# Projection matrices of a spectral mixer: scaled by ScalarE and summed by GpSimd, with the remainder ahead of the last square

## The chip, the cores and the metric

One core of a Trainium2 chip runs the kernel. The metric is the device time of one execution in microseconds (us), the median of several runs. The engines are named PE (TensorE, matrix products; PEld is its loading of weights), DVE (VectorE), ACT (ScalarE), POOL (GpSimd) and SP (SyncE, which issues the DMAs here). GpSimd and the DMAs work on SBUF; the results of matrix products stand in PSUM and are taken from there by VectorE and ScalarE.

## What is computed

The reference is a model of four layers on an image of 56 x 56 positions, 128 channels and a batch of 2: two layers of selective scans, an attention layer with a spectral mixer behind it, and an attention layer with experts. The change touches the mixer alone (`_L2_ffn_ref`), which convolves the tokens with 16 spectral filters, multiplies each result by a matrix, and does so for prefixes of the sequence of four lengths, each with matrices of its own:

```python
def _compute_spectral(u, sigma, phi, Mpp, Mpm):
    U_plus, U_minus = _stu_conv(phi, u, PADDED_SL)
    s = sigma ** SIGMA_POW
    out = jnp.einsum('btkd,k,kde->bte', U_plus, s, Mpp)
    out = out + jnp.einsum('btkd,k,kde->bte', U_minus, s, Mpm)
    return out
...
for i, frac in enumerate((1, 2, 4, 8)):
    xi = x[:, :T // frac]
    si = _stu(xi, sigma, phi, M_u[i], M_phi_plus[i], M_phi_minus[i])
    si = jnp.pad(si, ((0, 0), (0, T - si.shape[1]), (0, 0)))
    outs.append(si)
y_soft = jax.nn.softmax((log_weights + gumbel) / TEMPERATURE)
y_hard = jax.nn.one_hot(jnp.argmax(y_soft), 4, dtype=y_soft.dtype)
weights = y_hard - jax.lax.stop_gradient(y_soft) + y_soft
stacked = jnp.stack(outs, axis=-1)
return jnp.sum(stacked * weights, axis=-1)
```

## The kernel before

The kernel does the layers one after the other. In the mixer, even and odd positions are kept apart, so that the sum and the difference of the plus and the minus matrix of a filter act on even and odd taps. The four prefix lengths give four stretches of the sequence; in the stretch that only the longest prefix reaches one matrix acts, in the next the weighted sum of two, and so on. So for each filter the kernel needs eight matrices of 128 x 128, the tile `Wm`: two (sum and difference) for each of four stretches, each a running sum of matrices that are weighted by `ws` (a scale per filter and prefix, the same in all partitions).

`matrices(f)` (L1798) builds `Wm` for filter f: two DMAs bring the plus and minus matrices into `mpm`; GpSimd adds and subtracts them (L1803, L1804) into `both`; VectorE weights and sums them in four operations of 128 x 256 (`stretch_sums`, L1869 once and L1871 three times). `mpm` and `both` have one buffer, `Wm` has four.

The stage is 32 units: two passes, in each eight pairs of filters, and for each pair of filters two units (`eo` = 0 and 1). The two units with the same filters are called a pair here. A unit (`unit`, L1726) is four squares, which are fast convolutions of blocks. Each square (`square`, L1692) makes seven products on TensorE, each into one buffer named `cv` of a PSUM pool of six (`product`); ScalarE copies two of them out (`less`, L1708), VectorE combines them by nine operations with PSUM operands (L1711 to L1722), ScalarE makes four times a half (L1720), and GpSimd adds two halves (L1724). The squares are u0 from ("T", "A"), u2 from ("A", "A") and ("T", "B"), S from ("C", "C") and u1 from ("D", "D"). GpSimd then adds S to u2 (L1744) and to u1 (L1753). `project` multiplies a block by `Wm` on TensorE (L1823, tile `pj`, two buffers), and VectorE adds the result to `A` (L1829). The projection of u0 is written after the S square; those of u2, of the remainder's result and of u1 are left to the next unit (`waiting`, `finish`).

In the units with `eo` = 0 the `remainder` (L1765) follows: 26 matmuls of x with the last taps `H` (L1771) for both units of the pair, into one more `cv` buffer, and a copy by ScalarE into `rest` (L1776). It is written behind the D square.

`coming()` calls `matrices` for the next pair of filters in the unit with `eo` = 1, but a scheduler in the framework sets the order of each engine's instructions from what is ready: in the built program the work for the next pair stands in the unit with `eo` = 0, as soon as `Wm` buffers are free. Each engine then works through its own queue in that order. `inputs` (L1613) makes the transformed inputs vT, vA, vC and vD by VectorE, at the start and again at the change of pass; GpSimd makes part of their sources (L1630, L1632). `windows` (L1672) and `taps` load what the next units need.

Of the kernel before, what the change touches and what calls it, by code (L numbers as in the profile page):

```python
# [14 lines left out]
F32 = mybir.dt.float32  # L15
BF16 = mybir.dt.bfloat16
AF = mybir.ActivationFunctionType
ALU = mybir.AluOpType
# [6 lines left out]
C = 128  # L25
# [1564 lines left out]
class Mixer:  # L1590
# [135 lines left out]
    def unit(self, f0, eo, after, later, project, ready, coming):  # L1726

        nc = self.k.nc
        u0 = self.block("u0")
        self.square(u0, ("T", "A"))  # L1730
        self.finish(1)
        u2 = self.block("u2")
        self.square(u2, ("A", "A"), ("T", "B"))
        if after:
            self.windows("A", *after)
            self.windows("B", *after)
        self.finish()
        if ready:
            self.inputs("C")
        S = self.block("S")  # L1740
        self.square(S, ("C", "C"))
        if after:
            self.windows("C", *after)
        nc.gpsimd.tensor_tensor(u2, u2, S, ALU.add)  # L1744
        coming()
        project(u0, 0)
        if ready:
            self.inputs("D")
        u1 = self.block("u1")
        self.square(u1, ("D", "D"))  # L1750
        if after:
            self.windows("D", *after)
        nc.gpsimd.tensor_tensor(u1, u1, S, ALU.add)  # L1753
        if eo == 0:
            self.remainder()
        if later is not None:
            self.taps(later, eo)
        rest = self.rest[:, :, eo]
        self.waiting = [(u2, 8 * KB), (rest, NB * KB), (u1, 4 * KB)]
        self.project = project  # L1760
# [23 lines left out]
def layer2_mixer(k, d, given, last, win):  # L1784

    nc, A, ws = k.nc, given.A, given.ws  # L1790
    NF = 16
    with ExitStack() as ctx:
        mixer = Mixer(k, ctx, given, last, win)
        tp = ctx.enter_context(k.pool("tmix", 1))
        wp = ctx.enter_context(k.pool("wmix", 4))
        p2 = ctx.enter_context(k.pool("pproj", 2, psum=True))

        def matrices(f):  # L1798
            m = tp.tile([128, 2, 4, C], F32, name="mpm")
            for i, n in enumerate(("plus", "minus")):  # L1800
                nc.sync.dma_start(m[:, i], d["L2_M_phi_" + n][:, f].rearrange("i d e -> d i e"))
            both = tp.tile([128, 4, 2, C], F32, name="both")
            nc.gpsimd.tensor_tensor(both[:, :, 0, :], m[:, 0], m[:, 1], ALU.add)  # L1803
            nc.gpsimd.tensor_tensor(both[:, :, 1, :], m[:, 0], m[:, 1], ALU.subtract)  # L1804
            Wm = wp.tile([128, 2, 4, C], F32, name="Wm")
            stretch_sums(nc.vector, Wm.rearrange("p f r e -> p r f e"), both, lambda i: ws[:, i, f : f + 1])
            return Wm

        def project(Ws, eo, par):

            s = 1 if eo == 1 and par == 0 else 0
            edges = [0, L // 16, L // 8, L // 4, HL]

            def do(u, a0):
                end = min(a0 + u.shape[-1], HL - s)
                for c0 in range(a0, end, 512):
                    c1 = min(c0 + 512, end)
                    for b in range(B):
                        ps = p2.tile([128, 512], F32, name="pj")
                        for r in range(4):  # L1820
                            lo, hi = max(c0, edges[r] - s), min(c1, edges[r + 1] - s)
                            for f in range(2 if lo < hi else 0):
                                nc.tensor.matmul(  # L1823
                                    ps[:, lo - c0 : hi - c0], lhsT=Ws[f][:, eo, r, :], rhs=u[:, b, f, lo - a0 : hi - a0],
                                    start=f == 0, stop=f == 1,
                                )
                        t0 = 2 * (c0 + s) + par
                        out = A[:, b, t0 : t0 + 2 * (c1 - c0) - 1 : 2]
                        nc.vector.tensor_tensor(out, out, ps[:, 0 : c1 - c0], ALU.add)  # L1829

            return do

        units = [(pin, f0, eo) for pin in range(2) for f0 in range(0, NF, 2) for eo in range(2)]
        for eo in range(2):
            mixer.taps(0, eo)
        for name in SETS:
            mixer.windows(name, 0, 0)
        mixer.inputs("T")
        mixer.inputs("A")
        Ws = [matrices(f) for f in range(2)]  # L1840
        for n, (pin, f0, eo) in enumerate(units):
            given = []

            def coming():
                if eo == 1 and n + 1 < len(units):
                    if f0 == NF - 2:
                        mixer.inputs("T")
                        mixer.inputs("A")
                    given.extend(matrices((f0 + 2) % NF + f) for f in range(2))

            if (f0, eo) == (NF - 2, 1) and pin == 0:
                mixer.fetch()
            mixer.unit(
                f0, eo, units[n + 1][1:] if n + 1 < len(units) else None,
                units[n + 2][1] if n + 2 < len(units) else None, project(Ws, eo, pin ^ eo),
                (f0, eo) == (0, 0), coming,
            )
            Ws = given or Ws
        mixer.finish()
# [7 lines left out]
def stretch_sums(engine, out, m, weight):  # L1867

    engine.tensor_scalar_mul(out[:, 3], m[:, 0], weight(0))  # L1869
    for i in range(1, 4):  # L1870
        engine.scalar_tensor_tensor(out[:, 3 - i], m[:, i], weight(i), out[:, 4 - i], ALU.mult, ALU.add)  # L1871
# [288 lines left out]
def program(tc, d, out):  # L2160
    with ExitStack() as ctx:
        k = Chip(ctx, tc)
        dp = ctx.enter_context(tc.tile_pool(name="m2t", bufs=1, space=bass.MemoryType.DRAM))
        with ExitStack() as ctx3:
            with ExitStack() as ctx2:
                with k.pool("big") as bp:
                    pair = bp.tile([128, 2 * L], F32, name="pair")
                    big = [pair[:, 0:L], pair[:, L:]]
                    big += [bp.tile([128, n], F32, name=f"big{i}") for i, n in enumerate((L, NKT * C, L, NKT * C))]
                    attention = Attention2(k, big)  # L2170
                    with ExitStack() as ctx1:
                        heads = []

                        def follow(ctx):
                            heads.append(Layer1(k, ctx1, d, big))
                            return heads[0].start(ctx)

                        layer0(k, d, big, follow)
                        heads[0].run(attention.start)
                    A = ctx3.enter_context(k.pool("mixed", side="right")).tile([128, B, L], F32, name="A")  # L2180
                    with ExitStack() as early:
                        given = MixerInputs(k, ctx2, early, d, A, pair[:, 0:MU])
                        taps = attention.run(lambda: mixer_filters(k, d, dp), given)
                attention = Attention3(k, ctx3, d)
                layer2_mixer(k, d, given, *taps)
            experts = Experts(k, ctx3, d)
            attention.run(A, experts)
            experts.run(out)
# [17 lines left out]
```

## Time and profile before

| | us |
|---|---|
| median of 3 runs | 9000.04 (8999.0 to 9005.41) |
| the profiled execution | 9000.1 |
| its span, first to last instruction | 8998.3 |
| the mixer in it | from 6405 to 8052 |

From the page, the busy time of the engines over the span:

```profile
PE 8056.0 (90%) x31375; PEld 4938.9 (55%) x31375; DVE 6921.5 (77%) x7145; ACT 5162.3 (57%) x11035; POOL 6779.2 (75%) x4136
```

The columns of a group of instructions are: line, engine, operation, output and inputs by the program's names, their shapes, count, busy time in us, mean ns of one, and the idle time of the engine just before them with what ended it. A wait names the waiting line, the releaser, the total in us, how often it occurred, and the longest.

In a window of one pair of the mixer (99 us) the engines are busy as follows (us and number of instructions for PE, PEld, DVE, ACT and POOL; then TensorE's granted clock, the busy share of the DMA engines, GB/s):

```profile
6680.00:6779.00 99.00, 91.44 (x448) 79.24 (x447) 70.57 (x104) 18.16 (x25) 60.99 (x25) 0.97 0.35 95
```

### The profile page before, as it was taken

How to read it: one execution, taken by the hardware profiler on the slowest of the kernel's cores; microseconds unless marked ns; L12 is line 12 of the kernel's file. 1: busy time of each engine (PE TensorE's matmuls, PEld its weight loads, DVE VectorE, ACT ScalarE, POOL GpSimd, SP SyncE). 2: the span in 40 equal slices, each digit the busy share in tenths (PEclk: the TensorE clock that was granted, in tenths of full speed). 3: DMA queues.
4: the chain of work that ended last, by engine and by line, in shares of the span. 5: the costliest groups of instructions: out<-in, count | busy, mean ns of one | idle time of the engine just before them, and what ended most of it. 6: DMA issues, size and time to landing. Idle time of an engine off the chain costs nothing. (4 is left out here: it accounts for less than half of the span.)

```text
span 8998.3 us, 102947 instructions
## 1 busy us (share of the span) xinstructions
PE 8056.0 (90%) x31375; PEld 4938.9 (55%) x31375; DVE 6921.5 (77%) x7145; ACT 5162.3 (57%) x11035; POOL 6779.2 (75%) x4136
## 2 busy tenths in 40 slices
PE   8999999999997888888888888699798989989998
PEld 4555555555554444444445444355587868865555
DVE  8999988999988997996997899511577677765442
ACT  6888877888876776775776777433211111114331
POOL 5999987999977996996998799466566655655551
PEclk9999999999998998998998999699899989989999
DMA  5666654666645874774885687200233323320004
GB/s 149 216 219 211 210 166 149 218 216 211 211 146 160 222 217 114 221 219 113 217 218 151 180 219 214 41 3 3 70 88 97 101 83 95 91 58 8 15 1 136
DMA packets 846613, 1276.65 MB, mean 142 GB/s; under 512 B 182813, under 2 KB 504350, under 8 KB 846058
## 3 DMA queue, kind: packets, MB, share of 16 engines
q1 hardware_dynamic: 846058, 1270.07, 48.7%
q8 instruction: 248, 4.06, 0.2%
q14 instruction: 307, 2.51, 0.1%
HBM read 1230.00 MB, written 46.58 MB: 142 GB/s over the span
## 5 line engine op out<-in xcount | busy, mean ns | idle before, releaser
L492 POOL TENSOR_TENSOR p<-h,c 128x784 f32<-128x784 f32 x2048 | 3764.1, 1864 | 296.4 <-DVE h L401 145.8
L401 DVE TENSOR_TENSOR_SCAN h<-a,state,h 128x784 f32<-128x784 f32 x1200 | 2169.7, 1833 | 1.7 <-ACT a L381 1.6
L421 PE MATMUL acc<-p,center 128*128 128x392 f32 x4096 | 1493.8, 500 | 5.6 <-POOL p L492 5.4
L421 PE MATMUL acc<-p,ident 128*128 128x392 f32 x4096 | 1427.8, 492 | 0.5 <-POOL p L492 0.4
L476 DVE TENSOR_TENSOR h<-du,b 128x784 f32<-128x784 f32 x1152 | 1096.1, 951 | 235.3 <-PE b L407 216.8
L381 ACT ACTIVATE a<-delta,L1A 128x784 f32<-128x784 f32 x896 | 819.9, 915 | 429.1 <-DVE h L401 424.3
L421 PEld LDWEIGHTS acc<-p,ident 128*128 128x128 f32 x4096 | 746.6, 190 | 532.4 <-issue 31.6
L421 PEld LDWEIGHTS acc<-p,center 128*128 128x128 f32 x4096 | 742.2, 193 | 494.6 <-issue 24.7
L1220 POOL TENSOR_TENSOR total<-total,e 128x448 f32<-128x448 f32 (+1 forms) x644 | 734.5, 1140 | 328.4 <-ACT e L1209 288.6
L495 POOL TENSOR_TENSOR h<-du,b 128x784 f32<-128x784 f32 x448 | 831.9, 1857 | 0.0
L1209 ACT ACTIVATE e<-sc 128x448 f32<-128x448 f32 (+1 forms) x700 | 376.9, 542 | 722.4 <-PE sc L1207 592.2
L381 ACT ACTIVATE a<-delta,L0A 128x784 f32<-128x784 f32 x704 | 643.2, 914 | 170.3 <-DVE h L401 164.9
L407 PE MATMUL b<-three,sel 96*128 96x512 bf16 (+1 forms) x2304 | 584.9, 335 | 173.8 <-DVE h L476 102.7
L1724 POOL TENSOR_TENSOR u<-u,T 128x1024 f32<-128x1024 f32 x192 | 448.9, 2359 | 382.7 <-DVE u L1722 382.7
L401 DVE TENSOR_TENSOR_SCAN h<-a,h 128x784 f32<-128x784 f32 x400 | 702.6, 1774 | 4.0 <-ACT a L381 3.1
L359 ACT ACTIVATE X<-X,BT 112x128 f32<-112x128 f32 x2100 | 683.8, 391 | 0.2
L401 DVE TENSOR_TENSOR_SCAN h<-h,state,a 128x784 f32<-128x784 f32 x336 | 617.8, 1839 | 0.0
L1708 ACT ACTIVATE less<-cv 128x512 f32<-128x512 f32 x256 | 152.3, 595 | 650.3 <-PE cv L1686 619.9
L407 PEld LDWEIGHTS <-sel 96*128 96x128 bf16 x2304 | 225.0, 101 | 522.0 <-issue 366.0
L1720 ACT ACTIVATE T<-T 128x1024 f32<-128x1024 f32 x128 | 135.4, 1058 | 612.5 <-DVE T L1718 553.0
L359 ACT ACTIVATE big<-big,BT 112x64 f32<-112x64 f32 x1680 | 444.5, 335 | 0.0
L1823 PE MATMUL pj<-u,Wm 128*128 128x196 f32 (+8 forms) x1536 | 358.8, 387 | 22.4 <-POOL u L1744 15.6
(535 smaller groups left out, 14492.5 us busy)
## 6 DMA issues: line engine op xcount, KB each, us to landing
c<-rows SPq DMA_DIRECT2D x1024, 392.0 KB, 3.9
c<-rows SPq DMA_DIRECT2D x2048, 196.0 KB, 4.0
b<-rows SPq DMA_DIRECT2D x512, 196.0 KB, 4.4
b<-rows SPq DMA_DIRECT2D x192, 392.0 KB, 4.5
wA<-win SPq DMA_DIRECT2D x64, 448.0 KB, 4.9
wB<-win SPq DMA_DIRECT2D x64, 448.0 KB, 6.8
wC<-win SPq DMA_DIRECT2D x64, 448.0 KB, 5.0
wD<-win SPq DMA_DIRECT2D x64, 448.0 KB, 4.8
```

Of the source, the lines that this page charges most:

```text
L359: self.k.nc.scalar.activation(x["bT"][:, i, c0:c1], g["duT"][x["ci"]][:, i, c0:c1], AF.Copy, scale=g["BT"][:, r : r + 1])
L381: self.k.nc.scalar.activation(x["a"], g["delta"][ci], AF.Exp, scale=self.w["A"](g["kd"], ci, x["n"]))
L401: self.k.nc.vector.tensor_tensor_scan(h, a, b, start, ALU.mult, ALU.add)
L407: self.k.nc.tensor.matmul(ps[:, c0:c1], lhsT=self.w["selB"](x["n"]), rhs=x["g"]["three"][:, c0:c1], start=True, stop=True)
L421: nc.tensor.matmul(job["acc"][:, i, 0:392], lhsT=self.w["sum"], rhs=x["p"][:, 392 * i : 392 * (i + 1)], start=False, stop=n == NS - 1,)
L476: nc.vector.tensor_tensor(one["h"], one["g"]["du"][one["ci"]], one["b"], ALU.mult)
L492: nc.gpsimd.tensor_tensor(now["p"], now["h"], now["c"], ALU.mult)
L495: nc.gpsimd.tensor_tensor(three["h"], three["g"]["du"][three["ci"]], three["b"], ALU.mult)
L1209: nc.scalar.activation(e[:n], ps[:n], AF.Exp, scale=scale)
L1220: nc.gpsimd.tensor_tensor(total[:n], total[:n], e[:n], ALU.add)
L1724: nc.gpsimd.tensor_tensor(u[:, :, :, o], u[:, :, :, o], half, ALU.add)
L1823: nc.tensor.matmul(ps[:, lo - c0 : hi - c0], lhsT=Ws[f][:, eo, r, :], rhs=u[:, b, f, lo - a0 : hi - a0], start=f == 0, stop=f == 1,)
```

## The change

The `remainder` of the units with `eo` = 0 is written ahead of the D square, directly behind the projection of u0. `matrices` now scales the plus and minus matrices of each prefix by `ws` on ScalarE, in place, in four activations of 128 x 256; GpSimd makes the running sums in place, in three additions of 128 x 256, and then the sum and the difference for all four stretches, in two operations of 128 x 512, straight into `Wm`. VectorE has no part in it. `both` is gone and `mpm` has two buffers in its place. The stretches stand in `Wm` in the opposite order, which the index in `project` follows.

```diff
@@ unit
         project(u0, 0)
+        if eo == 0:
+            self.remainder()
         if ready:
             self.inputs("D")
         u1 = self.block("u1")
...
         nc.gpsimd.tensor_tensor(u1, u1, S, ALU.add)
-        if eo == 0:
-            self.remainder()
         if later is not None:
             self.taps(later, eo)
@@ layer2_mixer
-        tp = ctx.enter_context(k.pool("tmix", 1))
+        tp = ctx.enter_context(k.pool("tmix", 2))
...
         def matrices(f):
-            m = tp.tile([128, 2, 4, C], F32, name="mpm")
+            m = tp.tile([128, 4, 2, C], F32, name="mpm")
             for i, n in enumerate(("plus", "minus")):
-                nc.sync.dma_start(m[:, i], d["L2_M_phi_" + n][:, f].rearrange("i d e -> d i e"))
-            both = tp.tile([128, 4, 2, C], F32, name="both")
-            nc.gpsimd.tensor_tensor(both[:, :, 0, :], m[:, 0], m[:, 1], ALU.add)
-            nc.gpsimd.tensor_tensor(both[:, :, 1, :], m[:, 0], m[:, 1], ALU.subtract)
+                nc.sync.dma_start(m[:, :, i], d["L2_M_phi_" + n][:, f].rearrange("i d e -> d i e"))
+            for i in range(4):
+                nc.scalar.activation(m[:, i], m[:, i], AF.Copy, scale=ws[:, i, f : f + 1])
+            for i in range(1, 4):
+                nc.gpsimd.tensor_tensor(m[:, i], m[:, i], m[:, i - 1], ALU.add)
             Wm = wp.tile([128, 2, 4, C], F32, name="Wm")
-            stretch_sums(nc.vector, Wm.rearrange("p f r e -> p r f e"), both, lambda i: ws[:, i, f : f + 1])
+            nc.gpsimd.tensor_tensor(Wm[:, 0], m[:, :, 0], m[:, :, 1], ALU.add)
+            nc.gpsimd.tensor_tensor(Wm[:, 1], m[:, :, 0], m[:, :, 1], ALU.subtract)
             return Wm
@@ project
-                                    ps[:, lo - c0 : hi - c0], lhsT=Ws[f][:, eo, r, :], rhs=u[:, b, f, lo - a0 : hi - a0],
+                                    ps[:, lo - c0 : hi - c0], lhsT=Ws[f][:, eo, 3 - r, :], rhs=u[:, b, f, lo - a0 : hi - a0],
```

## The prediction

> **What bounds the kernel now.** The page's slices come first. TensorE is at 90% of the span, and the part that the change touches is the mixer, 6405 to 8052 us. There the waits view of TensorE (waiter, releaser: us in total, times, longest) is the next thing to read:
>
> ```profile
> PE cv L1771 <- DVE u L1712: 98.5, 13, 7.6
> PE cv L1686 <- issue: 24.2, 3, 12.2
> PE pj L1823 <- POOL u L1744: 15.6, 2, 13.3
> PE cv L1686 <- DVE vC L1641: 8.4, 1, 8.4
> ```
>
> One wait dominates: 13 times, always 7.6 us, TensorE stands at the remainder (L1771) until VectorE has finished L1712. It occurs in 13 of the 16 pairs of units; in the first pair and in the first of the second pass other waits come before it, and in the last one no matrices are left to build. What VectorE does meanwhile is in the timeline of one such place (start, duration, engine, line):
>
> ```profile
> 6763.11 2.26 DVE L1871 SCALAR_TENSOR_TENSOR Wm<-both,ws,Wm 128x256 f32<-128x256 f32 x1
> ...
> 6765.89 6.60 DVE L1871 SCALAR_TENSOR_TENSOR Wm<-both,ws,Wm 128x256 f32<-128x256 f32 x2
> 6767.66 4.56 POOL L1744 TENSOR_TENSOR u<-u,S 128x2048 f32<-128x2048 f32 x1
> 6772.42 0.68 DVE L1711 TENSOR_TENSOR u<-cv,less 128x512 f32<-128x512 f32 x1
> ...
> 6773.84 8.18 PE L1771 MATMUL cv<-H,x 128*128 128x128 f32 x52 [7.56 <-DVE u L1712]
> ```
>
> The D square's seven products are on TensorE from 6760.1 to 6766.3, but VectorE takes up the first of them only at 6772.4, because weight sums (L1871) stand ahead in its queue, and one of these, worth 0.48 us, lasts until GpSimd's 4.56 us add ends. The remainder is the eighth user of a six-buffer PSUM pool, so it waits for L1712 to free the D square's second product. The gap costs more than itself, as the windows (us; busy of PE, PEld, DVE, ACT, POOL; clock; DMA share; GB/s) show:
>
> ```profile
> 6760.00:6765.00 5.00, 5.00 (x26) 4.43 (x25) 5.00 (x7) 2.14 (x3) 2.26 (x1) 1.00 0.79 213
> 6765.00:6770.00 5.00, 1.28 (x6) 0.78 (x5) 4.96 (x4) 0.00 (x0) 4.92 (x3) 1.00 0.00 0
> 6770.00:6775.00 5.00, 1.16 (x5) 1.19 (x6) 5.00 (x6) 0.00 (x0) 4.64 (x3) 0.65 0.00 0
> 6775.00:6780.00 5.00, 5.00 (x33) 5.00 (x32) 3.48 (x6) 1.06 (x1) 1.52 (x2) 0.67 0.67 186
> ```
>
> The granted clock falls to about 0.65 and returns within some 5 us; the remainder, run in that time, takes 8.18 us. In the last pair, without a gap, it takes 5.97 us. Everywhere else in a pair TensorE is 5.00 of 5.00 us busy at clock 1.00: it is the bound, and these gaps are what can be had. The groups give the prices (busy us, mean ns | idle before):
>
> ```profile
> L1871 DVE SCALAR_TENSOR_TENSOR Wm<-both,ws,Wm 128x256 f32<-128x256 f32 x96 | 151.9, 1582 | 1.7
> L1771 PE MATMUL cv<-H,x 128*128 128x128 f32 x832 | 125.7, 326 | 98.5 <-DVE u L1712 98.5
> L1869 DVE TENSOR_SCALAR Wm<-both,ws 128x256 f32<-128x256 f32 x32 | 41.7, 1305 | 30.8 <-POOL both L1804 22.6 <-PE pj L1823 8.2
> L1804 POOL TENSOR_TENSOR both<-mpm 128x512 f32<-128x512 f32 x32 | 40.9, 1278 | 0.0
> ```
>
> [...] L1871 takes 469 ns at least and 4600 ns at most, L1869 339 to 2551 ns, while VectorE's work on PSUM stays at 0.67 to 0.69 us beside GpSimd. [...]
>
> **The change part by part.**
>
> *Weight sums leave VectorE.* 8 operations a pair go (2 L1869, 6 L1871): 193.6 us of VectorE over the stage, 12 us a pair. VectorE's 70.6 us in the pair from 6680 to 6779 become some 59 in 89; nothing waits on it but what already did, so its lateness in the D square goes.
>
> *The remainder goes ahead of the D square.* In TensorE's built order it now stands after the projection of u0 and before D. Its PSUM buffer is then that of the C square's second product, freed some 5 us earlier, and its matmuls run while VectorE drains the C square. No added instruction; H and x are loaded long before. On SP the reload of H now stands ahead of wD instead of behind it; wD is used some 35 us later. ScalarE's copy L1776 (0.37 us) moves with it. Cost: none.
>
> *Steady gain.* Idle 98.5 us, plus the slow clock: 125.7 us busy minus 16 x 5.97 = 30.2 us. Sum 128.7 us. Check: one pair lasts from the remainder at 6773.84 to the next at 6872.69, 98.85 us; less 7.57 and 2.3 is 89.0 us.
>
> *What is added.* ScalarE: 8 activations of 128x256 a pair, with a scale per partition. The nearest row is L359 with such a scale, 391 ns for 128 elements and 335 for 64, 0.875 ns an element, so 503 ns for 256; successive ones start some 0.1 us before the last ends: 0.40 us each, 3.3 us a pair, beside the 18.2 us of the same window. GpSimd: 6 sums of 256 a pair; between 1268 (512) and 2357 ns (1024) the slope is 2.13 ns, so 0.72 us each, 4.3 us; the 4 adds of 512 (5.1 us) stay in number. GpSimd goes from 61.0 us in that window to 65 in 89. None is a bound.
>
> *The new waits.* The built order of one eo = 0 unit, times from the start of its C square on TensorE (t = 0), with durations of the trace. GpSimd: u2's last adds end at 2.2 (6708.94 and 6706.46 + 4.68 in the unit before), then four adds to Wm, ending at 3.5, 4.7, 5.9 and 7.2. The second and fourth free the two mpm buffers, whose DMAs SP issues at once (0.37 + 0.51 us; 3.4 us to land, 6.0 at most): landed at 8.6 and 11.0. ScalarE: four scalings 8.6 to 10.3, S's activation L1720 (11.3), four scalings to 13.0. GpSimd: five sums to 13.6, then the S adds (4.67) to 18.3, one sum, L1744 to 23.5. TensorE: C to 6.1, u0's projection to 9.6, remainder to 15.4, D to 21.4, the next square to 27.5, and there u2's projection needs L1744: 4 us to spare. Behind ScalarE's second four stand L1776 (due at 15.5) and D's first "less" (17.4): 2.5 us to spare at the first, more at the second. With a landing of 6.0 us for both the chain is 2.6 to 5 us later, and a stall of about 1 us appears. So: 0, bounds 0 and 5 us a pair. The built order hoists sums for the pair after next, so nothing waits for Wm itself.
>
> *Start and change of pass.* At the start TensorE loses 12.2 + 2.6 us before D, which waits for vD on VectorE behind L1871 (5.04 us in one pair of them). In the new order the remainder (6.0 us) fills part, and the sums are gone; against it, six sets of matrices instead of four are scaled and summed on ScalarE and GpSimd before vD's input (L1632). Bounds +6 lost to 16 gained; I take 11 gained. At 7282 to 7295 TensorE waits 13.3 us for L1744; the remainder fills 6 of it and 2.6 us of L1871 go: 7, bounds 0 and 12.
>
> *Sum.* 128.7 + 11 + 7 = 147 us. The profiled execution took 9000.1 us with a span of 8998.3, and the median of the runs is 9000.04, so: 9000 - 147 = 8853 us, span 8851.
>
> **Rivals.** (A, the forecast) the gaps go: 8853; with the bounds of start and pass 8843 to 8877. (B) A new wait takes part back: the chain DMA, ScalarE, GpSimd in the eo = 0 unit runs past its 2.5 to 4 us. For it: it goes through four queues, and ScalarE's "less" stands behind it. Against it: the working above. At 3 us in each of 14 pairs, 8853 + 42 = 8895. (C) The gap only moves to the D square, because GpSimd and not VectorE is late: the change doesn't do what it says. For it: GpSimd gets more work ahead of S. Against it: GpSimd idles 382.7 us before L1724. About 8990. (D, slower) Without pauses TensorE is granted less clock. The place is the whole stage: the longest stretch without a gap is now 91 us, and will be some 700. Its 1430 us at clock c cost 1430 x (1/c - 1), which passes the gain of 147 and the 0.2% at c = 0.90; at 0.87 it is +214 and 9067. For it: weight loads are busier here than anywhere (79 of 99 us, against 218 of 420 in the attention stage). Against it: from 5890 to 6310 TensorE is busy 419.9 of 420 us at clock 1.00.
>
> **How the numbers follow.** A 0.76, B 0.15, C 0.04, D 0.05. The likeliest is A: 8853. The range reaches from 8838 (A's best case, a little below) through A and most of B to 8900. Under 0.2% (18 us) can't be told from no change here. Faster: A, B and half of C, 0.92; same: 0.03; slower: D, 0.05.
>
> **What would show it.** Right: no wait of L1771 for L1712; TensorE busy all of a pair; 89 us between two remainders; a remainder of 6.0 us at clock 1.00; no Wm row on VectorE. B shows as waits of u2's projection for L1744, or of "cv" for "less". D shows as a clock under 0.95 in windows without a gap. Wrong: pairs of 92 us or more, or a start that loses time.

## The result and the profile after

| | before, us | after, us |
|---|---|---|
| median of 4 runs | 8999.52 (8994.44 to 9005.41) | 8852.19 (8842.56 to 8861.42) |
| the profiled execution | 9000.1 | 8861.42 |
| its span | 8998.3 | 8859.6 |
| the mixer in it, first product of a square to last projection | 1646.8 (6405.7 to 8052.5) | 1508.0 (6412.9 to 7921.0) |

The ratio of after to before is 0.9836, 95% interval 0.9819 to 0.9853. A second comparison, in the last pair of experiments below, gave 0.9840 (0.9827 to 0.9854): 8860.63 against 9000.17 us. So the change takes 139 to 147 us off, and the mixer of the profiled execution accounts for 138.8 of them. Outside the mixer the code is the same. The profiled mixer starts 7.2 us later than before, and what follows it is 7.2 us shorter (938.6 against 945.8 us). In the eight profiled executions of this study the mixer starts anywhere from 6404.5 to 6413.0 us. That spread isn't explained here. So a difference of a few us between kernels is read from the mixer, not from the whole time.

The waits view of TensorE, in the changed kernel over the mixer (6390 to 7930 us; waiter, releaser: us in total, times, longest), has no line for the remainder any more:

```profile
PE cv L1686 <- issue: 24.5, 3, 12.0
PE pj L1825 <- POOL u L1744: 11.1, 2, 8.8
PE cv L1686 <- DVE vD L1641: 8.8, 1, 8.8
PE cv L1686 <- DVE u L1712: 6.0, 2, 5.5
PE pj L1825 <- POOL u L1724: 5.6, 1, 5.6
```

The 98.5 us of 13 equal waits are gone. What is left occurs once to three times; in the order of time it stands at the start and at the change of pass, not in the pairs. The groups view of the same window (busy us, mean ns | idle before) shows the remainder and the new operations:

```profile
L1771 PE MATMUL cv<-H,x 128*128 128x128 f32 x832 | 95.6, 276 | 0.0
L1805 POOL TENSOR_TENSOR mpm<-mpm 128x256 f32<-128x256 f32 x96 | 70.7, 737 | 57.6 <-ACT mpm L1803 52.8
L1803 ACT ACTIVATE mpm<-mpm,ws 128x256 f32<-128x256 f32 x128 | 54.3, 496 | 81.5 <-DMA mpm<-in_L_M_phi_minus_dram 81.4
```

The remainder's 832 matmuls take 95.6 us, 276 ns each, instead of 125.7 and 326. The new work takes 0.74 us a sum and 0.50 us a scaling, and both engines wait a good deal ahead of it, for the fetch of the matrices. Whether that wait reaches TensorE is seen in the order of time. This is the timeline of one unit with eo = 0 (start, duration, engine, line):

```profile
6739.89 1.28 POOL L1808 TENSOR_TENSOR Wm<-mpm 128x512 f32<-128x512 f32 x1
...
6742.59 1.71 ACT L1803 ACTIVATE mpm<-mpm,ws 128x256 f32<-128x256 f32 x4 [5.09 <-DMA mpm<-in_L_M_phi_minus_dram]
...
6743.64 5.98 PE L1771 MATMUL cv<-H,x 128*128 128x128 f32 x52
...
6745.72 1.70 ACT L1803 ACTIVATE mpm<-mpm,ws 128x256 f32<-128x256 f32 x4 [0.47 <-DMA mpm<-in_L_M_phi_minus_dram]
...
6748.19 4.66 POOL L1724 TENSOR_TENSOR S<-S,T 128x1024 f32<-128x1024 f32 x2
...
6749.65 0.37 ACT L1776 COPY rest<-cv 128x256 f32<-128x256 f32 x1 [2.22 <-PE cv L1771]
...
6753.50 4.55 POOL L1744 TENSOR_TENSOR u<-u,S 128x2048 f32<-128x2048 f32 x1
...
6761.54 3.60 PE L1825 MATMUL pj<-u,Wm 128*128 128x512 f32 x8
```

The C square of this unit starts at 6734.05. ScalarE is done with the scalings at 6747.4, t = 13.4, and waits 2.22 us for the remainder before L1776. L1744 ends at 6758.05, t = 24.0, and the projection that needs it starts at 6761.54, t = 27.5. The chain is there as worked out, with 2.2 and 3.5 us to spare, and TensorE doesn't feel it. Remainders now follow each other at 6743.64, 6832.53, 6921.42 and 7010.31 us: 88.89 us a pair. In windows of the stage (us; busy of PE, PEld, DVE, ACT, POOL; clock; DMA share; GB/s) TensorE has no gap in 510 us, and the clock stays whole:

```profile
6600.00:6700.00 100.00, 100.00 (x500) 87.09 (x499) 65.17 (x108) 23.71 (x36) 69.29 (x32) 1.00 0.40 112
7330.00:7840.00 510.00, 510.00 (x2525) 440.88 (x2524) 335.69 (x556) 117.38 (x176) 363.61 (x161) 1.00 0.37 99
```

### The profile page after: what moved, and what is told of

It is laid out like the page before. It is cut to its first block, busy times and chain, and to the rows that moved or that the text cites. A ratio compares the mean times of both kernels' runs of the same rounds, so it can differ in the third digit from the quotient of the medians.

```text
span 8859.6 us, 103132 instructions
## 1 busy us (share of the span) xinstructions
PE 8016.3 (90%) x31375; PEld 4917.8 (56%) x31375; DVE 6741.0 (76%) x7017; ACT 5213.9 (59%) x11163; POOL 6848.1 (77%) x4232
## 5 line engine op out<-in xcount | busy, mean ns | idle before, releaser
L1724 POOL TENSOR_TENSOR u<-u,T 128x1024 f32<-128x1024 f32 x192 | 448.8, 2358 | 263.6 <-DVE u L1722 263.3
```

The source lines that it names most:

```text
L1724: nc.gpsimd.tensor_tensor(u[:, :, :, o], u[:, :, :, o], half, ALU.add)
```

## The experiments

The change has two parts, and each could by itself explain the time: the remainder's new place, and the matrices' new engines. The first two experiments each do one of them. The texts on record speak of a lock where a sum lasts until an add of GpSimd ends. In the trace of the kernel before that is what the last sum ahead of each of the 13 waits does: it takes 4.60 us and ends 0.28 us after L1744, where the median sum takes 0.485 us.

### The remainder's place alone

The kernel before with:

```diff
         project(u0, 0)
+        if eo == 0:
+            self.remainder()
...
         nc.gpsimd.tensor_tensor(u1, u1, S, ALU.add)
-        if eo == 0:
-            self.remainder()
```

> The kernel before with the remainder ahead of the D square; the matrices stay as they were (sums on VectorE). My theory (VectorE takes up the D square's second product too late, at the same moment as before, because weight sums stand ahead of it and one of them is locked by GpSimd's L1744): the wait does not go with the remainder, it passes to the next square's first product, which now is the user of that PSUM buffer; TensorE comes to it 5.97 us later, so 1.6 us are left of 7.57, with no remainder at a low clock behind them. Pair of units 90.5 to 91 us, time 8885 to 8905 us. Rival 1 (place alone matters, and the wait goes whole): pair 89 us, 8855 to 8875 us. Rival 2 (the wait moves whole to another instruction): pair 98 to 99 us, 8980 to 9010 us.

Measured: 8880.92 us (8879.71 to 8884.37), ratio 0.9867 (0.9852 to 0.9882); mixer 1539.5 us; pair 91.9 us. One pair in its timeline (VectorE's and TensorE's lines):

```profile
6836.43 6.21 PE L1686 MATMUL cv<-wD,vD 128*128 128x256 f32 x28
6836.45 6.64 DVE L1871 SCALAR_TENSOR_TENSOR Wm<-both,ws,Wm 128x256 f32<-128x256 f32 x2
...
6843.01 0.68 DVE L1711 TENSOR_TENSOR u<-cv,less 128x512 f32<-128x512 f32 x1
...
6844.39 2.83 PE L1686 MATMUL cv<-wA,vT 128*128 128x256 f32 x12 [1.75 <-issue]
...
6848.02 2.18 PE L1686 MATMUL cv<-wA,vT 128*128 128x256 f32 x9 [0.80 <-DVE u L1718]
```

The two sums still take 6.64 us, VectorE still comes to the D square's second product at 6843, and the wait has passed to the next square, as expected. It ends with L1712 at 6844.28 although the profile calls it "issue". A second pause of 0.80 us, for VectorE's later work on the same square, was not in my working, so the pair is 91.9 and not 90.5 to 91. The time came out 4 us under my range all the same. In the profiled executions what lies outside the mixer is 8.5 us shorter here than in the kernel before; why is not shown. In the mixer the gain is 107.3 us, against 138.8 with the whole change. The remainder itself takes 95.6 us in all, as in the changed kernel, where the clock is 1.00. Both rivals (89 and 98 us a pair) fall.

### The matrices alone

The changed kernel with:

```diff
         project(u0, 0)
-        if eo == 0:
-            self.remainder()
...
         nc.gpsimd.tensor_tensor(u1, u1, S, ALU.add)
+        if eo == 0:
+            self.remainder()
```

> The changed kernel with the remainder back behind the D square; matrices scaled on ScalarE and summed on GpSimd. My theory (the lateness of VectorE is the whole cause): no wait of L1771 for L1712, pair 88.9 us as in the changed kernel; only the start loses what the remainder filled there, about 6 us: 8850 to 8868 us. Rival (the place of the remainder did it, the sums on VectorE were beside the point): L1771 still waits 5 us or more in each pair, pair 94 us or more, 8930 us or more.

Measured: 8870.92 us (8865.85 to 8877.77), ratio 0.9856 (0.9841 to 0.9870); mixer 1519.8 us; pair 88.9 us. The remainder's group in the mixer:

```profile
L1771 PE MATMUL cv<-H,x 128*128 128x128 f32 x832 | 95.6, 275 | 0.4 <-DVE u L1712 0.3
```

Of 98.5 us of waiting 0.3 are left, with the remainder where it was. So VectorE's lateness was the cause, and taking the sums off VectorE removes it. In the pairs the move adds next to nothing to that. What it is worth is 11.8 us of the mixer (1519.8 against 1508.0), nearly all at the start and the change of pass: the first unit takes 81.1 us instead of 75.9 (first square to the next unit's first), and at the change of pass a projection waits 14.9 us for L1744 instead of 8.8. I had put this at 6 us, so the time came out 3 us above my range.

### How VectorE's lateness is made up

The kernel before without one line:

```diff
-        nc.gpsimd.tensor_tensor(u2, u2, S, ALU.add)
```

> The kernel before without the add u2 += S (L1744), so the output lacks the share of the C square in one of the three parts. It parts the two halves of VectorE's lateness, the lock by L1744 and the weight sums queued ahead. My theory: the second of the two sums at the end no longer takes 4.6 us but 0.48, so L1712 comes some 4.2 us earlier and L1771 waits 3.2 us (2.5 to 4) instead of 7.57; if so short a pause leaves the clock whole, the remainder takes 6.0 us instead of 8.2: pair 92 to 95 us, time 8910 to 8950 us. Rival 1 (the queue of sums alone, no lock): L1771 waits 7 us or more, pair 98 us or more, 8985 us or more. Rival 2 (the lock alone): no wait left, pair 89 us, under 8880 us.

Measured: 8929.22 us (8918.93 to 8933.59), ratio 0.9919 (0.9903 to 0.9936); mixer 1572.5 us; pair 93.9 to 95.6 us. One pair (in this kernel the remainder is L1770 and the sums are L1870):

```profile
6733.10 1.00 DVE L1870 SCALAR_TENSOR_TENSOR Wm<-both,ws,Wm 128x256 f32<-128x256 f32 x2
...
6741.99 4.85 POOL L1724 TENSOR_TENSOR S<-S,T 128x1024 f32<-128x1024 f32 x2 [5.31 <-DVE S L1722]
...
6742.36 2.27 DVE L1870 SCALAR_TENSOR_TENSOR Wm<-both,ws,Wm 128x256 f32<-128x256 f32 x1
...
6745.15 2.50 DVE L1870 SCALAR_TENSOR_TENSOR Wm<-both,ws,Wm 128x256 f32<-128x256 f32 x2
6747.57 0.68 DVE L1711 TENSOR_TENSOR u<-cv,less 128x512 f32<-128x512 f32 x1
...
6748.99 8.86 PE L1770 MATMUL cv<-H,x 128*128 128x128 f32 x52 [3.46 <-DVE u L1712]
```

The two sums take 2.50 us instead of 6.60, and the wait falls from 7.57 to 3.46 us, against 3.2 worked out. So 4.1 us of each wait went with L1744, and 3.5 us came from the rest. Both rivals fall as they were stated, for the one with L1744 alone foresaw no wait at all.

The rest is not mainly the sums' own time, though. With GpSimd at rest two sums take 1.00 us (6733.10). At 6742.36 and 6745.15 three sums take 4.77 us, while L1724's two adds run from 6741.99 to 6746.84; so some 3.3 us of these are again time beside GpSimd, now L1724. In the kernel before the three sums at this place take 8.86 us (2.26 and 6.60 in the lines of the prediction), 7.4 us above their own time, which is nearly the whole wait of 7.57. In its trace, ahead of all 13 waits, the first takes 2.26 to 2.27 us and the second 1.97 to 1.98, and each ends 0.28 to 0.29 us after an add of L1724; the third ends 0.28 us after L1744. The runs show that the time goes with GpSimd's add; why the two go together they do not show. An estimate from these times: the sums with no add of GpSimd beside them would have left almost no wait. No run shows that.

The pause shrank but the remainder stayed slow: 124.5 us in all, hardly less than 125.7, where I had thought that so short a pause might leave the clock whole. Windows around the remainder of this pair, and around another of the same kernel, show the clock (it is the third figure from the end):

```profile
6745.60:6748.90 3.30, 0.00 (x0) 0.00 (x0) 3.27 (x5) 0.00 (x0) 2.36 (x2) 0.88 0.00 0
6749.00:6751.00 2.00, 2.00 (x9) 2.00 (x10) 2.00 (x4) 0.00 (x0) 1.27 (x2) 0.50 0.03 8
6751.00:6753.00 2.00, 2.00 (x12) 2.00 (x11) 2.00 (x5) 1.06 (x1) 0.00 (x0) 0.50 0.74 200
6753.00:6755.00 2.00, 2.00 (x11) 2.00 (x11) 0.63 (x2) 0.00 (x0) 1.29 (x1) 0.52 0.86 208
6755.00:6757.50 2.50, 2.50 (x25) 2.50 (x24) 0.00 (x0) 0.00 (x0) 2.50 (x2) 1.00 0.90 249
...
6557.00:6560.70 3.70, 0.28 (x2) 0.00 (x0) 3.67 (x5) 0.00 (x0) 2.77 (x2) 0.95 0.01 2
6560.80:6562.80 2.00, 2.00 (x10) 2.00 (x11) 2.00 (x4) 0.00 (x0) 1.22 (x1) 0.50 0.00 0
6562.80:6564.80 2.00, 2.00 (x15) 2.00 (x15) 2.00 (x5) 1.06 (x1) 0.00 (x0) 0.76 0.72 209
6564.80:6566.80 2.00, 2.00 (x20) 2.00 (x19) 0.57 (x1) 0.00 (x0) 1.35 (x1) 1.00 1.00 205
```

The clock records in the trace of the kernel before hold 1.00 and 0.50 and no other value. If that is so here too, the mean of a window tells when the clock changed. In the first pair the window of 3.30 us at 0.88 holds 0.8 us of half clock, so it fell at 6748.1, and it was whole again at 6754.9: 6.8 us. In the second it fell at 6560.3 and rose at 6563.8: 3.4 us. After pauses of nearly the same length, the remainders take 8.86 and 7.48 us. The last section comes back to this.

### The spare in the new chain

The changed kernel with:

```diff
-        tp = ctx.enter_context(k.pool("tmix", 2))
+        tp = ctx.enter_context(k.pool("tmix", 1))
```

> The changed kernel with one buffer for the fetched matrices (tmix 1) in place of two: the two sets of a pair go one after the other through DMA, ScalarE and GpSimd. My theory of the spare in the new chain (4 us ahead of L1744, 2.5 us ahead of L1776): the second set ends on GpSimd at about the time at which the S adds start anyway; the next set's scalings wait on ScalarE for their DMA until about 12 us after the start of the remainder and hold L1776 and the D square's less behind them: some 2 us a pair on TensorE, 20 to 50 us in all, 8870 to 8900 us. Rival 1 (the chain has much more spare than worked out): 8850 to 8860 us, no new wait of cv. Rival 2 (the chain has no spare, every us of it shows): 5 us a pair or more, over 8920 us.

Measured: 8880.15 us (8874.97 to 8889.26), ratio 0.9866 (0.9852 to 0.9881); mixer 1530.2 us; pair 90.6 to 92.2 us. TensorE's waits over the mixer, the lines that are new:

```profile
PE cv L1686 <- ACT rest L1776: 9.8, 12, 1.9
PE cv L1686 <- DVE u L1718: 9.6, 12, 0.8
```

and one of the places in the timeline:

```profile
6838.97 1.70 ACT L1803 ACTIVATE mpm<-mpm,ws 128x256 f32<-128x256 f32 x4 [7.16 <-DMA mpm<-in_L_M_phi_minus_dram]
...
6840.59 0.35 ACT L1776 COPY rest<-cv 128x256 f32<-128x256 f32 x1
...
6840.98 1.99 PE L1686 MATMUL cv<-wD,vD 128*128 128x256 f32 x8 [0.49 <-ACT rest L1776]
```

ScalarE stands 7.16 us at a scaling whose matrices are still on the way, and L1776 behind it comes when TensorE already wants the PSUM buffer. That is the place and the size I had expected: 2 us a pair, and 22.2 us of the mixer (1530.2 against 1508.0). So the spare in the pairs was real but small: a fetch that is issued 7.4 us later against the remainder (4.9 us after its start instead of 2.5 ahead of it) uses it up and costs 2 us more. The second buffer belongs to the change. At the start it does harm, however: with one buffer two sets instead of four stand ahead of the L1724 that `inputs("C")` waits for (next section), and the first unit takes 70.3 us instead of 75.9.

### What is left at the start

In the changed kernel the C square of the very first unit waits 12.0 us. VectorE's line at that place is

```profile
6452.85 2.27 DVE L1639 SCALAR_TENSOR_TENSOR T<-vC 128x1024 f32<-128x1024 f32 x1 [8.53 <-POOL u L1724]
```

L1639 writes f, the scratch of `inputs("C")`, into the block T4, and T4 is free only when GpSimd's L1724 has added it to u2. That add stands behind the sums of the third and fourth set of matrices in GpSimd's queue. The experiment gives the scratch of C and D blocks that are free at that time, and runs beside the changed kernel on the same chip. The edit is in `inputs`:

```diff
-            c = self.scratch("u0" if name == "D" else "u1", 7)
+            c = self.scratch("u1", 7)
...
-        f, g = self.scratch("T4", 4), self.scratch("T", 2)
+        if name in "CD":
+            fg = self.scratch("S" if name == "C" else "u0", 6)
+            f, g = fg[:, 0:4], fg[:, 4:6]
+        else:
+            f, g = self.scratch("T4", 4), self.scratch("T", 2)
```

> The changed kernel as it is, beside the next one on the same chip: 8840 to 8865 us, 0.982 to 0.986 of the kernel before; pair 88.9 us.

> The changed kernel with the scratch of the C and D inputs apart from the squares: f and g of C in the block of S, of D in that of u0, the differences of D in u1; nothing else changed. My theory of what is left of the pauses at the start (vC and vD wait in T4 for GpSimd, whose adds stand behind six sets of matrix sums): C's 12.0 us fall under 4 and D's 8.8 under 4, so the first unit is 10 to 18 us shorter; at the change of pass 0 to 6 us more. 8828 to 8842 us, 10 to 24 us under the changed kernel. Rival (GpSimd is full at the start, its queue sets the end of the first unit whatever VectorE does): the pauses go over to projections that wait for L1744 or L1755, gain under 5 us.

Measured: the changed kernel 8860.63 us (8851.93 to 8862.17), ratio 0.9840 (0.9827 to 0.9854), mixer 1508.2 us; with the scratch apart 8843.75 us (8838.40 to 8861.84), ratio 0.9828 (0.9814 to 0.9841), mixer 1499.6 us. The two intervals overlap, so the 17 us between the medians aren't settled; 8.6 us is what the mixer shows. It has the lowest median of the study, 2 us above my range. The first unit takes 66.8 us instead of 76.3, a little less of a gain than the 10 us or more that I had expected. Its timeline has these pauses of TensorE (products are L1690 here, scalings L1807, VectorE's L1714 is L1718):

```profile
6438.18 5.46 PE L1690 MATMUL cv<-wC,vC 128*128 128x256 f32 x12 [3.55 <-DVE vC L1650]
...
6461.74 2.04 PE L1690 MATMUL cv<-wD,vD 128*128 128x256 f32 x4 [8.64 <-ACT mpm L1807]
```

and ScalarE and VectorE ahead of the second:

```profile
6447.33 1.31 ACT L1807 ACTIVATE mpm<-mpm,ws 128x256 f32<-128x256 f32 x3 [8.69 <-DMA mpm<-in_L_M_phi_minus_dram]
6448.54 0.57 ACT L1712 ACTIVATE less<-cv 128x512 f32<-128x512 f32 x1
...
6449.20 0.69 DVE L1718 SCALAR_TENSOR_TENSOR T<-less,cv 128x512 f32<-128x512 f32 x1 [6.82 <-POOL Wm L1812]
```

C's pause fell as expected; D's did not. ScalarE waits 8.69 us for the fifth set of matrices, which is for the pair after next, the C square's second "less" stands behind, VectorE behind that (the profile names L1812, but the operand that came last is "less"), and vD is late. On the way to vD GpSimd takes its share too: L1644 and L1645 take 2.82 and 2.56 us beside GpSimd's adds, where the same operations (L1640 and L1641 in the changed kernel) take 0.68 and 0.42 us for vT at 6407. So my theory holds for C and fails for D: it isn't the scratch alone, the chain of DMA, ScalarE and GpSimd also binds in the first unit. At the change of pass the gain that I had allowed for did not come: outside the first unit the mixer is 0.9 us longer.

## Why the prediction was right

- **The bound and its cause.** The wait of the remainder for VectorE, 98.5 us, went entirely. The matrices alone remove all but 0.3 us of it, and without L1744 the wait is 3.46 us: late sums, which last until GpSimd's adds end, was the right cause. The prediction counted one such sum, of 4.6 us beside L1744; the other two at that place, of 2.26 and 1.97 us, end with L1724's adds as well.
- **The steady gain of 128.7 us.** Measured term by term 128.6: 98.5 us of waits and 125.7 - 95.6 = 30.1 of slow clock. Taken from the start of a unit to that of the next, the 13 units with the wait are 130.8 us shorter together. Pair 88.89 us against 89.0, remainder 5.98 us. The reading of the clock was too mild, though: 0.65 was the mean of a window, and the clock stood at half for 6.8 to 10.2 us and not for some 5 (last section). The sum did not suffer, because it took the loss from the remainder's measured time. What the prediction did not see is that the two parts are substitutes here: the move alone gives 107.3 us of the mixer and the matrices alone 127.0, both at once 138.8. The reason given under "The remainder goes ahead of the D square", that its buffer is free earlier, holds for the remainder only; the buffer that was late has another next user.
- **What is added.** Scalings 496 ns against 503, sums 0.74 us against 0.72. TensorE does not wait for them in a pair.
- **The new waits, at nothing.** Right in each pair, by the 2.2 and 3.5 us seen above against 2.5 and 4. That this was near is shown by the kernel with one buffer: there rival B happens, on L1776, for 2 us a pair.
- **Start and change of pass.** These two terms were mis-sized. The start was put at 11 us gained and gives 80.2 - 75.9 = 4.3. The move alone gives 6.9 (first unit 73.3 us); the matrices, which were to bring the rest because the sums leave VectorE, cost 2.6 instead. They put ScalarE's scalings and GpSimd's sums for later pairs ahead of the first unit's own adds. The text counted the six sets but not that L1724, behind four of them, frees the block into which `inputs("C")` writes; with one buffer, and two sets ahead of it, the first unit takes 70.3 us. The first unit of the second pass takes 80.6 us instead of 83.9, so 3.4 us are gained there, against 7; again the move alone gives more (76.6 us) and the matrices alone lose (85.8 us). The end gives the last 0.3 us. Both gains lie within the bounds that were set.
- **The sum.** 147 us predicted; 138.8 in the profiled mixer, 147.3 and 139.5 between the medians of the two comparisons. The prediction's 8853 lies within 1 us of the first median, and part of that is luck: by the trace the sum was 8 us too high, since start and change of pass together were put 10 us too high and the steady gain came out 2 us above its forecast.
- **Rivals C and D.** No pause of the D square in the pairs, and a clock of 1.00 over 510 us without a gap. A is what happened.

## What to carry to other kernels

A wait for a PSUM buffer belongs to the engine that drains the pool late: moving the waiting product passes the wait, less the work that comes in between, to the next user of the buffer (here 7.57 us became 1.75 and 0.80, with 5.97 us of work between), while taking the delay off the draining engine removed it. A sum of two SBUF operands ahead of the drain in its queue cost 2.0 to 4.6 us here, until GpSimd's add ended, and not its own 0.5 us. When work moves to the queues of other engines, look for its cost at the start and at changes of pass, where it is hoisted ahead of adds that free a shared block, and not only in the steady loop.

## What the runs showed of the hardware

The length of TensorE's pause does not by itself set what the slow clock costs. Worked out from the means of windows as above, the clock was halved for 3.4 and 6.8 us after two pauses of 3.5 us without L1744. Of the kernel before, two pauses of 7.6 us read like this:

```profile
6771.00:6773.80 2.80, 0.00 (x0) 0.00 (x0) 2.80 (x4) 0.00 (x0) 2.44 (x2) 0.59 0.00 0
...
6777.80:6779.80 2.00, 2.00 (x18) 2.00 (x17) 0.68 (x2) 0.00 (x0) 1.24 (x1) 0.87 1.02 281
...
7396.00:7398.00 2.00, 0.00 (x0) 0.00 (x0) 2.00 (x1) 0.00 (x0) 2.00 (x1) 0.53 0.00 0
...
7404.90:7406.90 2.00, 2.00 (x13) 2.00 (x13) 0.65 (x2) 0.00 (x0) 1.27 (x1) 0.63 1.04 227
```

The first stretch runs from 6771.5 to 6778.3, 6.8 us, the second from 7396.1 to 7406.4, 10.3 us. The clock records of that trace have it so in all 13 waits: four stretches of 6.83 us and nine of 10.24. Without L1744, nine of the 13 remainders stand whole on a line of a timeline. Five take 7.38 to 7.67 us and four 8.86 to 9.00, so they are of the two kinds that the windows show (7.48 us with 3.4 us of half clock, 8.86 with 6.8).

Nor does the clock fall at a fixed time after the pause begins. Here are two more waits of 7.6 us in the kernel before:

```profile
6863.65:6867.07 3.42, 1.46 (x7) 0.95 (x5) 3.38 (x4) 0.00 (x0) 3.34 (x3) 1.00 0.00 0
6867.07:6870.48 3.41, 0.00 (x0) 0.00 (x0) 3.41 (x1) 0.00 (x0) 3.41 (x1) 1.00 0.01 2
6870.48:6873.89 3.41, 1.20 (x6) 1.23 (x7) 3.41 (x6) 0.00 (x0) 3.05 (x3) 0.50 0.00 0
...
6962.65:6966.06 3.41, 1.37 (x7) 0.87 (x5) 3.38 (x4) 0.00 (x0) 3.33 (x3) 1.00 0.03 7
6966.06:6969.47 3.41, 0.00 (x0) 0.00 (x0) 3.41 (x1) 0.00 (x0) 3.41 (x1) 0.50 0.00 0
```

In the first TensorE stops at 6865.1 and the clock falls at 6870.5, 5.4 us later; in the second it stops at 6964.0 and the clock falls at 6966.1, 2.0 us later. By the clock records the four stretches of 6.83 us begin 4.4 to 5.4 us after the pause does, and the nine of 10.24 us 2.0 to 2.8 us after. What decides between them is not shown.

A pause of 1.75 us (the remainder's move alone) left the clock at 1.00. A pause cut from 7.6 to 3.5 us saved its own 4 us and hardly anything of the slow clock: the remainders took 124.5 us in all without L1744 and 125.7 in the kernel before, against 95.6 in the changed kernel.
